# A table rewritten for its first sixteen strips ahead of the first pass over it

## The chip, the cores and the metric

The kernel runs on one core of a Trainium2 chip. A core has five engines with queues of their own: TensorE (PE, matmuls; its weight loads are shown as PEld), VectorE (DVE), ScalarE (ACT), GpSimd (POOL) and SyncE (SP, which here only issues DMAs). Sixteen DMA engines move data between device memory and the on-chip memory, whichever queue has issued the transfer. The metric is the time of one execution on the device in microseconds, as the median of several runs.

## The reference

A layer of a graph network: 12500 nodes with 128 features, 200000 edges sorted by their target `dst`, four types of edges with a weight matrix and a bias each.

```python
h = jnp.maximum(_layernorm(x, axis=-1), 0.0)
# edge by edge, with xs = h[src]:
for i in range(W.shape[0]):
    mask = (edge_types == i)[:, None]
    msgs = msgs + jnp.where(mask, xs @ W[i] + b[i], 0.0)
out = x + jax.ops.segment_sum(msgs, dst, num_segments=N)
```

The targets are drawn as a square of a uniform number, so low nodes have very many edges and high nodes few.

## The kernel before, in words

**Two ways to the sums.** The edges stand in 1563 chunks of 128. The first 576 chunks go to the few heavy targets and are done densely: for a target and a type, it is counted how often each of the 12500 sources occurs, and the counts are multiplied with the table of `h`. The other 987 chunks are gathered: POOL fetches the 128 rows of a chunk from the table by an indirect DMA (L622, tile `hm`, ten buffers of two chunks), PE sums them by a one-hot matrix (L675), weighs the sums with the four matrices (L701), and DVE adds them to a ring of output columns (L764). Groups have 16 chunks and eight parts of two chunks; the first three groups use rows of `x` instead of the table (tile `hx`, the "raw" groups, L733 and L746).

**Two tables.** `h` is written first, as `htab` in device memory: for each node 128 numbers in three 16-bit parts (one float16, two bfloat16), 768 bytes. Gathers read `htab`. The dense passes, but for the first, read a second table, `dtab`: the float16 part and the two others added up as one 32-bit number, 768 bytes too. The table is cut into 98 blocks of 128 nodes, three blocks to a strip: 33 strips of 288 KB (the last is shorter).

**Dense work** goes by batches of targets: the first batch has 29 units (three targets each), eighteen have 31. `count` makes a batch's counts: DVE builds two one-hot matrices for a slot of 128 edges (L1103, L1113), PE multiplies them (L1138), ACT casts the result into the tile `counts` (L1146). Each count has three 8-bit digits in one 32-bit word. `multiply` then makes a pass over the table for the batch, while the next batch is counted. In a pass over `dtab`, two strips form a run: six matmuls with the float16 part and the counts read as 8-bit floats (L1252), then six with the 32-bit part and the counts decoded by ACT (L1206 in `decode`, tile `dec`, L1244). In the first pass, each block takes three matmuls with the three 16-bit parts and the 8-bit counts (L1274) and no decoding.

**Where `dtab` comes from.** The first pass makes it on its way: when a strip has been multiplied, `keep` copies its float16 part on ACT (L1220), adds the other two on DVE (L1221), both into a buffer of the pool `decp` (four buffers, the same in which counts are decoded), and issues the store on ACT's queue (L1222), one strip late. Strips are loaded by SP into seven buffers `hs` (L1263 in the first pass, L1237 later). The pool of these buffers was opened in `end_raws`, at the end of the raw groups' work. At the end of a pass ACT copies the product, `sd` (L1290).

**Order.** PE, DVE and ACT run in the order in which the program is written. The loop over groups (from group 3, `gi == RAW`) writes it: at each of the eight parts of a group it takes as much dense work as `pace` allows. The pace counts columns of matmuls: a batch's counting and pass have a price in columns (`counting_columns`, `passing_columns`), and all of it is spread over 57 groups so that each group with its own columns has the same sum, some 34 thousand dense columns a group, 37 thousand in the narrow early ones. A pass costs `3 * units * PARTS * NW * NT` columns, with FIRST_PASS in place of PARTS for the first. Counting of the first batch, with 29 slots, has no pass beside it and is priced at ALONE = 3.5 times its columns, 39.8 thousand. By the plan it ends in group 4; the first pass and the counting of batch 1 begin there. In `dense_work`, a pass is opened by three calls of its generator (one decode each where it decodes); the first stands ahead of the next batch's first slot, and the pass trails that batch's counting by BEHIND = 0.15.

```python
for n in range(DECS - 1):
    decode(n)
    if n:
        settle(sds)
    yield 0.0
```

Of the kernel before, what the change touches and what calls it, by code (L numbers as in the profile page):

```python
# [36 lines left out]
BF16 = mybir.dt.bfloat16  # L37
F16 = mybir.dt.float16
F8 = mybir.dt.float8e4
F32R = mybir.dt.float32r  # L40
# [4 lines left out]
ALU = mybir.AluOpType  # L45
# [5 lines left out]
P = 128  # L51
# [7 lines left out]
UB = 31  # L59
MANY = 16  # L60
HB = 3
# [17 lines left out]
RUN = 2  # L79
UP = 4096.0  # L80
PARTS = 2.05
FIRST_PASS = 4.4
ALONE = 3.5
RAW_WORK = 20000.0
RAW_ADDS = 12
# [4 lines left out]
def kernel(  # L90
# [1093 lines left out]
    checks = []  # L1184

    sds = []

    def multiply(now):
        vs, counts = now
        nu = len(vs)  # L1190

        first = vs is batches[0]
        table = (htab if first else dtab).rearrange("(p j) f -> p j f", j=NW)
        split = dtab.rearrange("(p j) f -> p j f", j=NW)
        nv = 3 * nu * NT
        by_digit = counts.bitcast(U8)
        counts = counts.bitcast(F8)
        parts = [(j0, min(j0 + HB, NW)) for j0 in range(0, NW, HB)]
        decoded = {}

        def decode(n):
            j0, j1 = n * DS, min(n * DS + DS, NW)
            if first or j0 >= NW:
                return
            decoded[n] = decp.tile([P, DS, 3 * UB * NT], F32R, name="dec")
            nc.scalar.activation(  # L1206
                decoded[n][:, : j1 - j0, :nv].rearrange("p j (m v) -> p j m v", m=3),
                by_digit[:, j0:j1, : nu * NT * 4].rearrange("p j (v m) -> p j m v", m=4)[:, :, :3, :],
                AF.Copy,
                scale=2.0**-9,  # L1210
            )

        stores = []

        def keep(n, hs):
            j0, j1 = parts[n]
            both = decp.tile([P, DS, 3 * UB * NT], F32R, name="dec").rearrange("p j v -> p (j v)")
            both = both[:, : HB * D3 // 2].rearrange("p (j f) -> p j f", j=HB)[:, : j1 - j0]
            rest = hs.bitcast(BF16)[:, : j1 - j0]
            nc.scalar.copy(both.bitcast(F16)[:, :, :D], hs[:, : j1 - j0, :D])  # L1220
            nc.vector.tensor_tensor(both[:, :, D // 2 :], rest[:, :, D : 2 * D], rest[:, :, 2 * D :], ALU.add)  # L1221
            stores.append(lambda: nc.scalar.dma_start(split[:, j0:j1, :], both.bitcast(F16)))  # L1222
            if len(stores) > 1:
                stores.pop(0)()

        for n in range(DECS - 1):
            decode(n)
            if n:
# [1 line left out]
            yield 0.0  # L1230
        pa = a_ps.tile([P, 512], F32, name="pa")
        to = pa[:, :nv]
        for n in range(0, 0 if first else len(parts), RUN):
            run = []
            for j0, j1 in parts[n : n + RUN]:
                hs = rooms[2].tile([P, HB, D3], F16, name="hs")
                nc.sync.dma_start(hs[:, : j1 - j0, :], table[:, j0:j1, :])  # L1237
                run += [(j, hs[:, j - j0, :]) for j in range(j0, j1)]
            for c in (0, 1):
                if n + RUN + c not in decoded:  # L1240
# [17 lines left out]
                        )  # L1258
                if run[-1][0] + c < NW:
                    yield (run[0][0] + len(run) * (1 + c) / 2) / NW  # L1260
        for n, (j0, j1) in enumerate(parts if first else ()):
            hs = rooms[2].tile([P, HB, D3], F16, name="hs")
            nc.sync.dma_start(hs[:, : j1 - j0, :], table[:, j0:j1, :])  # L1263
            for ja in range(j0, j1, DS):
                js = range(ja, min(ja + DS, j1))
                todo = []
                for j in js:
                    of = counts[:, j, : nu * NT * 4].rearrange("p (v m) -> p m v", m=4)[:, :3, :]
                    todo.append((0, j, hs[:, j - j0, :D], of))
                    for c in (1, 2):  # L1270
                        todo.append((c, j, hs.bitcast(BF16)[:, j - j0, c * D : (c + 1) * D], of))
                todo.sort(key=lambda one: one[0])
                for n_done, (c, j, left, right) in enumerate(todo):
                    nc.tensor.matmul(  # L1274
                        to.rearrange("p (m v) -> p m v", m=3),
                        left,
                        right,
                        start=(j == 0 and c == 0),
                        stop=(js[-1] == NW - 1 and n_done == len(todo) - 1),
                    )  # L1280
                if js[-1] + 1 < NW:
                    yield (js[-1] + 1) / NW
            keep(n, hs)
        for store in stores:
            store()
        sds.append(lambda: end())

        def end():
# [309 lines left out]
    for gi, (t0, g) in list(enumerate(zip(starts, sizes)))[RAW:]:  # L1598
# [234 lines left out]
```

## Time and profile before

| | us |
|---|---|
| median of 3 runs | 1305.66 |
| the runs | 1305.32, 1305.66, 1309.93 |
| the profiled execution | 1311.28 |
| its span, first to last instruction | 1309.6 |
| first matmul of the first pass (L1274) | 164.5 |
| its copy `sd` | 247.6 |
| last copy `sd`, of the nineteenth batch | 1276.5 |

The page of the profile gives busy time by engine, the span in 40 equal slices of about 33 us (each digit the busy share in tenths), the chain of work that ended last, and groups of equal instructions with their line, tile names, number, busy time, mean duration in ns, and the idle time of the engine ahead of them with what ended it. The timeline lists instructions in order of time: start, duration, engine, line, operation, output and input, and in brackets the idle time before it. The window view gives each engine's busy time in a stretch, with the granted PE clock and the mean share of the DMA engines. "issue" is idle time for which the profile shows no cause.

### The profile page before, as it was taken

The page shows a single profiled execution, that of the slowest core. Times are in us where ns is not written, and L with a number is a line of the kernel's source. Part 1 is how long each engine was busy: PE and PEld are TensorE (multiplying, and loading weights), DVE is VectorE, ACT ScalarE, POOL GpSimd, SP SyncE. Part 2 cuts the span into 40 slices and gives each one's busy share as a digit, 9 for nine tenths or more (in the row PEclk, how much of TensorE's full clock was granted, in tenths as well). Part 3 has the DMA queues.
Part 4 walks back from the last instruction along what each step waited for, and adds up shares of the span by engine and source line. Part 5 has one row for each costly group of instructions (what it writes and reads, how often), then busy time and mean ns, then how long its engine had stood idle before and what let it go on. Part 6 is the DMA issues. An engine that isn't in the chain of part 4 may idle for free.

```text
span 1309.6 us, 30266 instructions
## 1 busy us (share of the span) xinstructions
PE 1227.2 (94%) x9190; PEld 878.9 (67%) x9190; DVE 1072.4 (82%) x5214; ACT 1064.0 (81%) x1814; POOL 954.0 (73%) x1028
## 2 busy tenths in 40 slices
PE   4887898799999999999999999999999999999996
PEld 1345655577777777777777776777777777777775
DVE  8996487897898987989888887879888797978454
ACT  6795644498988989899898988889888898888881
POOL 6727577777777777777777777777777777777772
PEclk9895689799999999999999999999999999999998
DMA  8644289888888888888787877878788788787982
GB/s 252 215 172 145 60 253 335 287 281 254 268 270 253 258 273 259 260 256 275 245 268 243 286 236 254 259 231 276 235 269 250 242 268 252 254 246 242 290 277 83
DMA packets 184229, 321.75 MB, mean 246 GB/s; under 512 B 30100, under 2 KB 82253, under 8 KB 184061
## 3 DMA queue, kind: packets, MB, share of 16 engines
q1 hardware_dynamic: 132701, 214.63, 50.2%
q0 software_dynamic: 46608, 95.52, 25.6%
q10 hardware_dynamic: 4752, 9.64, 1.9%
q8 instruction: 72, 1.18, 0.4%
q14 instruction: 96, 0.79, 0.2%
HBM read 293.99 MB, written 25.67 MB: 244 GB/s over the span
## 4 chain that ended last, share of the span: by engine, by line
PE 81%; ACT 8%; DVE 6%; DMA 2%; issue 2%; SPq 0%; DVEq 0%; ACTq 0%
PE pa L1244 22%; PE pa L1252 22%; PE pt L1138 11%; PE py L701 8%; PE ps L675 7%; ACT dec L1206 2%; PE pt L1297 2%; DMA dtab<-dec 1%; PE pa L1274 1%; DVE ring L764 1%; ACT h L540 1%; PE ps L733 1%; DVE o L1103 1%; PE pt L986 1%; DVE o L1113 1%
## 5 line engine op out<-in xcount | busy, mean ns | idle before, releaser
L622 POOL DMA_INDIRECT hm<-htab,srcT x939 | 900.8, 959 | 311.6 <-issue 194.1
L1206 ACT ACTIVATE dec<-counts 128x1116 fp32r<-128x1116 uint8 (+1 forms) x594 | 676.1, 1162 | 10.2 <-PE pa L1244 7.6
L1103 DVE TENSOR_SCALAR o<-iota_w,hkT 128x392 bf16<-128x392 f16 x1051 | 429.3, 408 | 114.8 <-PE pt L1138 113.3
L1244 PE MATMUL pa<-dec,hs 128*128 128x372 f32 x1764 | 389.9, 355 | 0.0
L1252 PE MATMUL pa<-counts,hs 128*128 128x372 fp8e4 x1764 | 342.5, 327 | 7.8 <-ACT sd L1290 7.8
L1146 ACT CAST counts<-pt 128x396 int32<-128x396 f32 x587 | 292.1, 523 | 39.5 <-PE pt L1138 15.2
L1244 PEld LDWEIGHTS pa<-dec,hs 128*128 128x128 f32 x1764 | 302.3, 188 | 15.6 <-issue 0.3
L1138 PE MATMUL pt<-o,o 128*128 128x396 bf16 x1051 | 280.1, 338 | 12.9 <-DVE o L1113 11.3
L1252 PEld LDWEIGHTS <-hs 128*128 128x128 f16 x1764 | 165.3, 97 | 121.3 <-issue 12.3
L1113 DVE TENSOR_SCALAR o<-iota_b,loT,byT 128x128 bf16<-128x128 bf16 x746 | 245.5, 329 | 0.0
L764 DVE TENSOR_TENSOR ring<-ring,py 128x14 f32 (+6 forms) x912 | 158.4, 174 | 58.0 <-issue 13.0
L665 ACT ACTIVATE sb<-ps 128x224 f32<-128x224 f32 (+7 forms) x235 | 102.6, 437 | 104.7 <-PE py L701 87.5
L675 PEld LDWEIGHTS <-hm 128*128 128x128 f16 x2817 | 142.9, 99 | 66.4 <-issue 13.3
L675 PE MATMUL ps<-oh,hm 128*128 128x56 bf16 (+7 forms) x2817 | 174.0, 198 | 1.6 <-DMA hm<-htab,srcT 1.6
L640 DVE TENSOR_SCALAR oh<-iota_b,keyT 128x56 bf16<-128x56 bf16 (+7 forms) x939 | 161.0, 261 | 6.8 <-PE ps L675 6.8
L701 PE MATMUL py<-sb,wsb 128*128 128x224 f32 (+6 forms) x456 | 122.3, 412 | 0.0
L1138 PEld LDWEIGHTS <-o 128*128 128x128 bf16 x1051 | 82.3, 98 | 55.5 <-DVE o L1113 16.0
L701 PEld LDWEIGHTS py<-sb,wsb 128*128 128x128 f32 x456 | 83.3, 193 | 26.4 <-ACT counts L1146 4.3
L1113 DVE TENSOR_SCALAR o<-iota_b,loT 128x128 bf16<-128x128 bf16 x305 | 83.0, 272 | 0.0
L606 POOL DMA_INDIRECT hx<-in_x_dram,srcT x48 | 46.8, 974 | 22.6 <-issue 9.3
L1274 PE MATMUL pa<-counts,hs 128*128 128x348 fp8e4 x294 | 53.0, 325 | 0.4 <-DMA hs<-htab 0.4
L696 ACT CAST cnt<-pt 128x224 bf16<-128x224 f32 (+10 forms) x61 | 25.7, 421 | 26.1 <-PE pt L692 24.5
(253 smaller groups left out, 789.8 us busy)
## 6 DMA issues: line engine op xcount, KB each, us to landing
hs<-dtab SPq DMA_DIRECT2D x576, 288.0 KB
hm<-htab,srcT POOLq DMA_INDIRECT x939
htab<-h SPq DMA_DIRECT2D x32, 288.0 KB
hs<-htab SPq DMA_DIRECT2D x32, 288.0 KB
dtab<-dec ACTq DMA_DIRECT2D x32, 288.0 KB
xo<-in_x_dram SPq DMA_DIRECT2D x23, 256.0 KB
out_dram<-xo SPq DMA_DIRECT2D x23, 256.0 KB
hm<-in_x_dram SPq DMA_DIRECT2D x18, 192.0 KB
```

Of the source, the lines that this page charges most:

```text
L622: one = nc.gpsimd.indirect_dma_start(out=hm[:, (i - h0) * D3 : (i - h0 + 1) * D3], out_offset=None, in_=htab, in_offset=bass.IndirectOffse ...
L640: nc.vector.tensor_scalar(oh[:, i, :], iota_b[:, :K], keyf[:, at : at + 1], None, ALU.is_equal)
L675: nc.tensor.matmul(ps[:, i - i0, :], rows(i, c), oh[:, i, :], start=(c == 0), stop=(c == 2))
L701: nc.tensor.matmul(py[:, :g, :], wsb[:, t, :], sb[0][:, :g, t, :], start=False, stop=(t == NT - 1))
L764: nc.vector.tensor_tensor(to, to, of(i), ALU.add)
L1103: one = nc.vector.tensor_scalar(o2[:, k, :NB].rearrange("p (r n) -> p r n", r=ROWS), iota_w, hkT[:, s : s + 1], None, ALU.is_equal)
L1113: one = nc.vector.tensor_scalar(o1[:, k], iota_b, loT[:, s : s + 1], by, ALU.is_equal, ALU.mult)
L1138: one = nc.tensor.matmul(pb, o1, o2, start=first, stop=last)
L1146: lambda i=i, pb=pb: nc.scalar.copy(counts[:, :, i * NT : (i + 1) * NT], pb.rearrange("p (b t) -> p b t", t=NT))
L1206: nc.scalar.activation(decoded[n][:, : j1 - j0, :nv].rearrange("p j (m v) -> p j m v", m=3), by_digit[:, j0:j1, : nu * NT * 4].rearrange(" ...
L1244: nc.tensor.matmul(to.rearrange("p (m v) -> p m v", m=3), row.bitcast(F32R)[:, D // 2 :], decoded[j // DS][:, j % DS, :nv].rearrange("p (m ...
L1252: nc.tensor.matmul(to.rearrange("p (m v) -> p m v", m=3), row[:, :D], counts[:, j, : nu * NT * 4].rearrange("p (v m) -> p m v", m=4)[:, :3 ...
```

## The change

A generator `rewrite` loads the first 16 strips of `htab` and rewrites them into `dtab` before the first pass, by the same `keep`. The loop over groups calls it once per part, from group 3 on; a call loads one strip and rewrites the strip loaded four calls earlier. The last of its twenty calls also issues the last store. When `multiply` is started for the first batch, it runs what is left of the generator to its end, ahead of its first decode. The first pass then takes strips 0 to 15 from `dtab`, in runs of two strips with decoded counts as later passes do, and strips 16 to 32 from `htab` in three parts as before, rewriting each behind its matmuls. The pool `hsp` is opened beside `decp`, before the loop over groups. The price of the first pass in `pace` falls from 4.4 to 3.6.

```diff
-FIRST_PASS = 4.4
+FIRST_PASS = 3.6
+EARLY = 16
+AHEAD = 4
...
+    strips = [(j0, min(j0 + HB, NW)) for j0 in range(0, NW, HB)]
+    stores = []
...
+    def keep(j0, j1, hs):
+        both = decp.tile([P, DS, 3 * UB * NT], F32R, name="dec").rearrange("p j v -> p (j v)")
+        both = both[:, : HB * D3 // 2].rearrange("p (j f) -> p j f", j=HB)[:, : j1 - j0]
+        rest = hs.bitcast(BF16)[:, : j1 - j0]
+        nc.scalar.copy(both.bitcast(F16)[:, :, :D], hs[:, : j1 - j0, :D])
+        nc.vector.tensor_tensor(both[:, :, D // 2 :], rest[:, :, D : 2 * D], rest[:, :, 2 * D :], ALU.add)
+        stores.append(lambda: nc.scalar.dma_start(blocks_of(dtab)[:, j0:j1, :], both.bitcast(F16)))
+        if len(stores) > 1:
+            stores.pop(0)()
+
+    def rewrite():
+
+        coming = []
+        for n in range(EARLY + AHEAD):
+            if n < EARLY:
+                j0, j1 = strips[n]
+                hs = hsp.tile([P, HB, D3], F16, name="hs")
+                nc.sync.dma_start(hs[:, : j1 - j0, :], blocks_of(htab)[:, j0:j1, :])
+                coming.append((j0, j1, hs))
+            if n >= AHEAD:
+                keep(*coming.pop(0))
+            yield True
+        stores.pop(0)()
...
         first = vs is batches[0]
+        for _ in writing if first else ():
+            pass
+        straight = EARLY if first else len(strips)
...
-            if first or j0 >= NW:
+            if n >= straight:
                 return
...
-        for n in range(0, 0 if first else len(parts), RUN):
+        for n in range(0, straight, RUN):
...
-        for n, (j0, j1) in enumerate(parts if first else ()):
+        for j0, j1 in strips[straight:]:
...
+            keep(j0, j1, hs)
...
     decp = counting.enter_context(tc.tile_pool(name="decp", bufs=DECS, side="right"))
+    hsp = counting.enter_context(tc.tile_pool(name="hsp", bufs=STREAM, side="right"))
+    writing = rewrite()
...
-        rooms.append(counting.enter_context(tc.tile_pool(name="hsp", bufs=STREAM, side="right")))
...
             late, tails[:] = list(tails), []
+            next(writing, None)
             while work and spent < pace(gi, part):
```

More of the change, by code (lines that the diff above doesn't have):

```diff
@@ L1197, in multiply @@
         counts = counts.bitcast(F8)
-        parts = [(j0, min(j0 + HB, NW)) for j0 in range(0, NW, HB)]
         decoded = {}
@@ L1211, in decode @@
             )
[L1213 to L1224, printed above, removed]
         for n in range(DECS - 1):
@@ L1260, in multiply @@
                     yield (run[0][0] + len(run) * (1 + c) / 2) / NW
-        for n, (j0, j1) in enumerate(parts if first else ()):
[L1262 to L1283, printed above, removed]
+        for j0, j1 in strips[straight:]:
+            hs = hsp.tile([P, HB, D3], F16, name="hs")
+            nc.sync.dma_start(hs[:, : j1 - j0, :], blocks_of(htab)[:, j0:j1, :])
+            todo = []
+            for c in range(3):
+                for j in range(j0, j1):
+                    left = hs.bitcast(BF16) if c else hs
+                    todo.append((left[:, j - j0, c * D : (c + 1) * D], counts[:, j, : nu * NT * 4].rearrange("p (v m) -> p m v", m=4)[:, :3, :]))
+            for i, (left, right) in enumerate(todo):
+                nc.tensor.matmul(
+                    to.rearrange("p (m v) -> p m v", m=3), left, right, start=False, stop=(j1 == NW and i == len(todo) - 1)
+                )
+            if j1 < NW:
+                yield j1 / NW
+            keep(j0, j1, hs)
         for store in stores:
             store()
+        stores.clear()
         sds.append(lambda: end())
```

10 lines of the change are left out of this document (5 added, 5 removed).

## The prediction, made before the changed kernel was run

> **What bounds the kernel now.** I read the page first, for what is busy all the time.
>
> ```profile
> span 1309.6 us, 30266 instructions
> PE   4887898799999999999999999999999999999996
> POOL 6727577777777777777777777777777777777772
> L622 POOL DMA_INDIRECT hm<-htab,srcT x939 | 900.8, 959 | 311.6 <-issue 194.1
> L675 PE MATMUL ps<-oh,hm 128*128 128x56 bf16 (+7 forms) x2817 | 174.0, 198 | 1.6 <-DMA hm<-htab,srcT 1.6
> L701 PE MATMUL py<-sb,wsb 128*128 128x224 f32 (+6 forms) x456 | 122.3, 412 | 0.0
> ```
>
> PE is at nine tenths from the eighth slice on. POOL never goes over seven, which looks like room. The timeline of POOL says otherwise, so it came second; then the window view of the gathers.
>
> ```profile
> 168.23 0.94 POOL L622 DMA_INDIRECT hm<-htab,srcT  x1 [0.55 <-PE ps L675]
> ...
> 1286.71 0.94 POOL L622 DMA_INDIRECT hm<-htab,srcT  x1 [0.30 <-DVE flag L893]
> 1287.96 0.95 POOL L622 DMA_INDIRECT hm<-htab,srcT  x1 [0.30 <-issue]
> ```
>
> ```profile
> 80.00:168.20 88.20, 51.46 (x48) 0.65 0.35 106
> 168.20:1290.00 1121.80, 849.39 (x891) 0.99 0.83 260
> ```
>
> A gather starts every 1.25 us: 0.95 of work and 0.30 that nothing shortens. From 168.23 on, 891 starts have 890 gaps, 1112.5 us at that pace, and took 1119.7. So POOL works without a break to 1288.9 and loses 7 us on the way. **PE and POOL bound the kernel together**; POOL may run 20 gathers (ten buffers of two) ahead of L675. The wait of 0.55 at 168.23 is the last that PE imposes: until then POOL is held back by PE, and what delays PE there delays POOL's whole row.
>
> Third, the window view by stages: counting of batch 0 (up to the first matmul of the first pass), strips 1 to 16, strips 17 to 33, what follows up to the copy `sd`, and a steady stretch for comparison. Columns: PE, PEld, DVE, ACT, POOL busy (instructions), granted clock, DMA share, GB/s.
>
> ```profile
> 150.60:164.50 13.90, 9.03 (x69) 4.94 (x68) 13.55 (x60) 10.56 (x28) 10.55 (x12) 0.87 0.28 76
> 164.50:201.50 37.00, 34.52 (x293) 21.91 (x292) 31.48 (x153) 15.99 (x41) 28.47 (x28) 0.90 0.84 265
> 201.50:238.40 36.90, 31.60 (x291) 20.95 (x290) 26.88 (x124) 15.46 (x40) 28.43 (x28) 1.00 1.00 347
> 238.40:247.60 9.20, 3.47 (x22) 1.27 (x19) 7.00 (x31) 3.98 (x7) 6.97 (x8) 0.59 0.99 327
> 350.00:450.00 100.00, 99.01 (x796) 73.72 (x795) 91.08 (x447) 91.64 (x146) 75.59 (x81) 1.00 0.84 264
> ```
>
> Counting of batch 0 is bound by DVE (13.55 of 13.90), with DMA at a share of 0.28. The second half of the pass is bound by DMA (share 1.00). The steady stretch is full on PE and over 90% on ACT and DVE.
>
> **Rewriting ahead: strips 0 to 9.** Loads, copies, adds and stores are the same instructions, moved. Keeps 0 to 3 stand at parts 4 to 7 of group 3, keeps 4 to 9 at parts 0 to 5 of group 4, by one step per part and a lag of four.
>
> ```profile
> 150.57 0.42 DVE L1103 TENSOR_SCALAR o<-iota_w,hkT 128x392 bf16<-128x392 f16 x1 [13.86 <-PE pt L1138]
> ...
> 177.19 0.55 DVE L1221 TENSOR_TENSOR dec<-hs 128x384 fp32r<-128x384 bf16 x1
> ```
>
> ```profile
> 168.10 0.51 ACT L1220 COPY dec<-hs 128x384 f16<-128x384 f16 x1
> 168.50 0.50 ACT L1146 CAST counts<-pt 128x396 int32<-128x396 f32 x1
> ...
> 169.56 0.37 ACTq L1222 DMA_DIRECT2D dtab<-dec  x1
> ```
>
> Keeps 0 to 3 lie in the 13.86 us that DVE waits in group 3: nothing, and 2 us if their copies held up the raw groups' evictions on ACT. Keeps 4 to 9 fall into 150.6 to 164.5. An add takes DVE 0.47 (the chain's piece below), a copy ACT 0.40 (168.10 to 168.50) and a store's issue 0.37. Six keeps are 2.8 us of DVE and 4.6 of ACT, whose own idle there is 3.3. I take DVE's **2.8**; bounds 0 and 4.6.
>
> **The drain.** `multiply` empties the rest of the generator before its first decode. Batch 0's counting ends at 39.8 thousand columns; the pace allows 39.2 before part 5 of group 4, where 14 of 20 steps are done. So six keeps (10 to 15) come in one block. Behind them in order are decode 0 on ACT, the casts of batch 1's slots, and on PE the fifth slot and the first matmul of the pass. Four buffers `dec` serve six keeps and the decodes, so copy 14 waits until store 10 has landed.
>
> ```profile
> 164.20 0.51 PE L1138 MATMUL pt<-o,o 128*128 128x396 bf16 x1 [0.45 <-DVE o L1113]
> 164.51 2.82 PE L1274 MATMUL pa<-counts,hs 128*128 128x348 fp8e4 x9
> 167.53 0.42 PE L675 MATMUL ps<-oh,hm 128*128 128x48 bf16 x6
> ```
>
> ```profile
> 176.32 0.15 PE ps L675 x6
> ...
> 192.21 4.65 DMA dtab<-dec
> ...
> 232.60 0.47 DVE dec L1221
> ```
>
> ```profile
> 255.90 2.16 ACT L1206 ACTIVATE dec<-counts 128x1116 fp32r<-128x1116 uint8 x2 [0.41 <-PE pa L1244]
> ```
>
> From the last one-hot for batch 1's slots (now about when the pass starts): add 10 0.47, store 10 0.37, landing, copy 14 and copy 15 with a store between them 1.17, two stores 0.74, decode 0 1.08, a cast 0.40, a slot 0.17: 4.4 us and a landing. No row shows a landing with quiet queues. From below, 288 KB at the 347 GB/s of the third stage are 0.85 us; from above stands the 4.65 in the full queue. DMA is at 0.28 here; I take 2.8, in the middle: **7.2 us**, bounds 5.3 and 9.1. [...]
>
> So the pass starts at about 174.5, 10 us later. PE is idle for most of it.
>
> **Strips 0 to 15 in two parts.** The chain's pieces give the matmuls at full clock.
>
> ```profile
> 173.52 1.38 PE pa L1274 x9
> 174.99 1.33 PE py L701 x8
> ...
> 253.98 0.99 PE pa L1252 x6
> 255.29 1.02 PE pa L1244 x6
> ```
>
> A strip costs PE 1.38 now, and three of each new kind 0.50 and 0.51: 16 strips fall from 22.1 to 16.1, 6.0 us saved. Left out besides are 16 adds (7.5 of DVE), copies and issues (12.3 of ACT). Added are 16 decodes, 17.3 of ACT. ACT's 15.99 become 26.9 (less 6.4 for copies; issues are not counted as busy). At the 91.64% that ACT reaches when PE is full, that is 29.4 us in place of 37.0: **-7.6**, bounds -6.0 (PE's saving alone) and -10.1 (ACT without a gap). DMA hides: the reads move from `htab` to `dtab`, the stores are gone.
>
> **Strips 16 to 32 and the end** keep their instructions, 46.1 us (201.5 to 247.6), DMA-bound. They start without the stores of strips 1 to 16 in the queue and have about 0.4 group less among them. I take **-2.5**; bounds 0, since the bytes of these strips are the same, and -8 (nine transfers of 288 KB less in the queue, at the 347 GB/s of that stage).
>
> **Pace.** FIRST_PASS down by 0.8 takes 27.3 thousand columns out of a plan of 37 thousand per early group, so 0.74 group fewer stands beside the pass and comes later. A group's sums are 8 x 0.15 and 1.33, 2.5 us early; over the run 174.0/2817x48 + 122.3/456x8 = 5.1. **+2**, bounds 1.9 and 3.8.
>
> **Sum:** 2.8 + 7.2 - 7.6 - 2.5 + 2 = +1.9 us: span 1311.5. The profiled execution took 1311.28 around its span of 1309.6, above the median of 1305.66; the change is put on the median, which gives **1307.6**, no difference that a measurement of this kernel tells from none (about 0.5%, 6.5 us).
>
> **Does POOL allow it?** L675 at 167.53 comes after the first half run (1.0) and moves by 8; POOL has no slack there, so its row moves by 8. Some of its 7 us loss comes back.
>
> ```profile
> 177.14 1.45 POOL L622 DMA_INDIRECT hm<-htab,srcT  x1 [0.31 <-issue]
> 178.90 0.94 POOL L622 DMA_INDIRECT hm<-htab,srcT  x1 [0.30 <-DMA hm<-htab,srcT]
> ...
> 1297.94 0.31 PE L675 MATMUL ps<-oh,hm 128*128 128x104 bf16 x3
> ```
>
> The gather at 177.14 is 0.5 longer, just beside the add at 177.19. Half the adds now meet a waiting POOL: 3 back of 7, bounds 0 and 7. The Trainium skill, "SBUF — State Buffer", section "SBUF: two separate sides", says that a DVE operation in a two-port mode locks GpSimd out of writing descriptors; the trace agrees with these two rows. POOL then ends 5 us later. Today 10.0 us lie between the start of the last gather and the last L675; 0.95 and a landing of 2.8 are needed, so 6.2 are free. POOL does not bind the forecast, but from about 1 us faster than before it would.
>
> **Rivals.** *Faster: a short drain.* Keeps 4 to 9 hidden (0), landing 0.85 (5.3), strips 0 to 15 at -10.1, the rest at -8, pace +2: -10.8. POOL's row then moves by 3.3, less 3, and the last L675 cannot come before 1290.1: at best -7.8. That gives 1297.9. For it: DMA at 0.28 before the pass. Against: ACT's queue stands still at every wait for a store.
>
> *Slower: ACT's queue.* It holds copies, store issues behind adds, decodes and casts in order. Landing at 4.65 (+1.9), keeps 4 to 9 at ACT's price (+1.8) and strips 0 to 15 at -6.0 (+1.6) give +7.2, 1312.9. It decides from a landing of about 4 us. For it: ACT is over 90% busy wherever it decodes. Against: quiet queues.
>
> *The change doesn't do what it says:* strips 0 to 15 stay at 37 us because ACT's decodes take what PE saves. +9.5, 1315.2. Against: the steady loop is the same code at a full PE. Its 19 copies `sd` (18 passes between) show the rate:
>
> ```profile
> L1290 ACT ACTIVATE sd<-pa x19: 442/473/502, 247.6 to 1276.5; 128x372 f32<-128x372 f32 x18, 128x348 f32<-128x348 f32 x1
> ```
>
> 57.2 us for 33 strips, 1.73 each, 27.7 for 16.
>
> **Chances.** Forecast 0.53, faster rival 0.22, ACT's queue 0.20, no gain in the pass 0.05. Faster by over 0.5%: 0.20 (the first rival but 0.02); slower: 0.24 (the last two but 0.02, and 0.01 of the forecast); within: 0.56. The range goes from the short drain to the last rival: 1298 to 1316, with one in ten left out at each end.
>
> **What would show it.** Right: first L1252 of the first pass near 174.5; a block of six copies on ACT with waits for `dtab` stores ahead of it; POOL waiting some 8 us for L675 between 165 and 176; sixteen strips in about 29 us; `sd` near 247.5; a lead of POOL at the end of about 7 us in place of 10. Wrong: a pass that starts before 170, or DVE and ACT stalls in strips 0 to 15 that leave PE under 85%. If the strips 16 to 32 run under 30 us, the backlog was worth more than I gave it.

## The result, and the profile after

The changed kernel took 1315.87 us in the median (1314.48 to 1317.85, 8 runs), the kernel before in the same set 1309.26 (1305.32 to 1312.3, 8 runs): a ratio of 1.0055, 95% interval 1.0038 to 1.0071. Forecast was +1.9 us, no difference that can be told; the change costs 6.6 us. Every later ratio is to the kernel before in its own set. (e1 to e18 are the runs below.) The three sets e1 to e4, e13 to e16, and e17 with e18 ran on two of the four chips that the sets had, where the kernel before takes 1574 to 1576 us because PE stands still every few microseconds; their times are compared only among themselves.

From the page of the changed kernel, the rows that answer to those of before:

```profile
span 1314.7 us, 30217 instructions
PE   4887769799999999999999999999999999999996
POOL 6737547777777777777777777777777777777773
L624 POOL DMA_INDIRECT hm<-htab,srcT x939 | 897.1, 955 | 323.6 <-issue 193.2
L677 PE MATMUL ps<-oh,hm 128*128 128x56 bf16 (+7 forms) x2817 | 173.4, 198 | 0.0
```

(L624, L677, L1115, L1140, L1148 are the lines that stood two higher in the kernel before; the copy, the add and the store of `keep` are now L1199, L1200, L1201, the decode L1237, the matmuls L1270, L1262 and, in three parts, L1288, the copy `sd` L1301.) PE does less, with a hole in its fifth and sixth slices (7 and 6 where 8 and 9 stood). The window view, by stages: from the last row of the raw groups (the copy at 149.3) to the first matmul of the first pass, to the first `sd`, to the last `sd`, to the end. The columns are those of the prediction.

```profile
149.30:177.20 27.90, 8.63 (x63) 4.78 (x61) 22.29 (x83) 15.70 (x39) 14.17 (x14) 0.67 0.92 307
177.20:246.70 69.50, 59.38 (x521) 41.35 (x519) 55.05 (x271) 41.73 (x84) 50.81 (x53) 0.92 0.90 299
246.70:1281.50 1034.80, 1016.26 (x7876) 747.93 (x7877) 859.86 (x4209) 905.96 (x1409) 782.80 (x828) 1.00 0.82 257
1281.50:1314.70 33.20, 20.41 (x176) 16.06 (x173) 14.99 (x78) 4.93 (x12) 10.97 (x12) 0.86 0.32 88
```

The same stages in the kernel before:

```profile
151.00:164.50 13.50, 8.63 (x65) 4.60 (x63) 13.15 (x59) 10.16 (x28) 10.15 (x12) 0.88 0.29 78
164.50:247.60 83.10, 69.59 (x602) 44.13 (x600) 65.36 (x306) 35.42 (x86) 63.87 (x63) 0.91 0.93 308
247.60:1276.50 1028.90, 1015.21 (x7844) 747.80 (x7845) 861.02 (x4202) 906.51 (x1406) 778.63 (x821) 1.00 0.83 258
```

The first stage grew by 14.4 us, the pass fell by 13.6, the long stretch of eighteen passes grew by 5.9. In the first stage PE works the same 8.63 us; DVE has 9.1 us more, and DMA, at 0.29 before, is at 0.92: the rewriting's own loads and stores fill the queues (5 and 12 are issued in this stage), and with them seven loads of strips that the pass will read. What ACT waits for in that stage is in its view of waits (line, releaser: total, times, longest):

```profile
ACT dec L1199 <- DMA dtab<-dec: 6.3, 4, 2.8
ACT counts L1148 <- PE pt L1140: 2.7, 1, 2.7
ACT counts L1148 <- DVE dec L1200: 2.7, 1, 2.7
ACT dec L1199 <- DVE dec L1200: 2.1, 1, 2.1
ACT dec L1237 <- DMA dtab<-dec: 1.0, 1, 1.0
```

Copies wait 6.3 us for stores that free their buffers, decode 0 another 1.0; 4.8 us are waits for an add on DVE, by which ACT's queue is held at a store. The chain that ended last shows one such landing (the time from a store's issue until its bytes have arrived) whole, and what stands behind it up to the pass:

```profile
168.43 0.35 ACTq L1201
...
168.90 4.88 DMA dtab<-dec
173.86 0.52 ACT dec L1199
174.41 0.57 DVE dec L1200
175.00 0.35 ACTq L1201
...
175.40 1.07 ACT dec L1237
176.47 0.39 ACT counts L1148
...
176.90 0.49 PE pt L1140
177.39 0.87 PE pa L1270 x3
```

A landing is 4.88 us where I took 2.8. While PE is out, POOL fills its ten buffers and stops:

```profile
166.49 0.95 POOL L624 DMA_INDIRECT hm<-htab,srcT  x1 [0.30 <-issue]
180.03 0.94 POOL L624 DMA_INDIRECT hm<-htab,srcT  x1 [12.60 <-PE ps L677]
...
1294.87 0.94 POOL L624 DMA_INDIRECT hm<-htab,srcT  x1 [0.30 <-issue]
```

### The profile page after: what moved, and what is told of

The parts are those of the page before. It is cut to its first block, busy times and chain, and to the rows that moved or that the text cites. A ratio compares the mean times of both kernels' runs of the same rounds, so it can differ in the third digit from the quotient of the medians.

```text
span 1314.7 us, 30217 instructions
## 1 busy us (share of the span) xinstructions
PE 1214.9 (92%) x9142; PEld 874.2 (66%) x9142; DVE 1072.0 (82%) x5214; ACT 1076.8 (82%) x1830; POOL 950.9 (72%) x1028
## 4 chain that ended last, share of the span: by engine, by line
PE 78%; ACT 8%; DVE 7%; DMA 4%; issue 2%; DVEq 0%; SPq 0%; ACTq 0%
PE pa L1262 22%; PE pa L1270 21%; PE pt L1140 11%; PE py L703 8%; PE ps L677 7%; ACT dec L1237 3%; DMA dtab<-dec 2%; PE pt L1308 2%; DVE ring L766 1%; DVE o L1105 1%; DVE o L1115 1%; PE ps L735 1%; ACT counts L1148 1%; ACT h L542 1%; PE pt L988 1%
## 5 line engine op out<-in xcount | busy, mean ns | idle before, releaser
L624 POOL DMA_INDIRECT hm<-htab,srcT x939 | 897.1, 955 | 323.6 <-issue 193.2
L1237 ACT ACTIVATE dec<-counts 128x1116 fp32r<-128x1116 uint8 (+2 forms) x610 | 696.1, 1163 | 9.0 <-DMA dtab<-dec 6.1
L1262 PE MATMUL pa<-dec,hs 128*128 128x372 f32 (+1 forms) x1812 | 400.6, 355 | 0.2 <-ACT dec L1237 0.2
L1270 PE MATMUL pa<-counts,hs 128*128 128x372 fp8e4 (+1 forms) x1812 | 351.8, 327 | 11.2 <-ACT sd L1301 9.6
L1262 PEld LDWEIGHTS pa<-dec,hs 128*128 128x128 f32 x1812 | 310.8, 189 | 16.3 <-issue 0.8
L1148 ACT CAST counts<-pt 128x396 int32<-128x396 f32 x587 | 295.2, 524 | 28.7 <-PE pt L1140 13.2
L1140 PE MATMUL pt<-o,o 128*128 128x396 bf16 x1051 | 279.2, 337 | 29.3 <-DVE o L1115 17.1
L1270 PEld LDWEIGHTS <-hs 128*128 128x128 f16 x1812 | 169.8, 97 | 136.5 <-issue 14.5
L1115 DVE TENSOR_SCALAR o<-iota_b,loT,byT 128x128 bf16<-128x128 bf16 x746 | 244.0, 327 | 0.0
L677 PEld LDWEIGHTS <-hm 128*128 128x128 f16 x2817 | 141.7, 99 | 63.7 <-issue 13.7
L677 PE MATMUL ps<-oh,hm 128*128 128x56 bf16 (+7 forms) x2817 | 173.4, 198 | 0.0
L1140 PEld LDWEIGHTS <-o 128*128 128x128 bf16 x1051 | 83.4, 98 | 63.0 <-DVE o L1115 22.6
L703 PEld LDWEIGHTS py<-sb,wsb 128*128 128x128 f32 x456 | 83.1, 193 | 24.6 <-ACT dec L1199 2.0
L1115 DVE TENSOR_SCALAR o<-iota_b,loT 128x128 bf16<-128x128 bf16 x305 | 82.7, 271 | 0.0
L698 ACT CAST cnt<-pt 128x224 bf16<-128x224 f32 (+10 forms) x61 | 25.7, 422 | 30.9 <-PE pt L694 29.1
L542 ACT ACTIVATE h<-hm,nmrt,rstdt 128x128 f32<-128x128 f32 x98 | 42.2, 491 | 1.1 <-DVE nmrt L537 1.0
```

Source lines behind the costliest of these rows:

```text
L624: one = nc.gpsimd.indirect_dma_start(out=hm[:, (i - h0) * D3 : (i - h0 + 1) * D3], out_offset=None, in_=htab, in_offset=bass.IndirectOffse ...
L677: nc.tensor.matmul(ps[:, i - i0, :], rows(i, c), oh[:, i, :], start=(c == 0), stop=(c == 2))
L703: nc.tensor.matmul(py[:, :g, :], wsb[:, t, :], sb[0][:, :g, t, :], start=False, stop=(t == NT - 1))
L1115: one = nc.vector.tensor_scalar(o1[:, k], iota_b, loT[:, s : s + 1], by, ALU.is_equal, ALU.mult)
L1140: one = nc.tensor.matmul(pb, o1, o2, start=first, stop=last)
L1148: lambda i=i, pb=pb: nc.scalar.copy(counts[:, :, i * NT : (i + 1) * NT], pb.rearrange("p (b t) -> p b t", t=NT))
```

## The experiments

A first table, of the profiles of the two sets that ran like the first comparison, and of the two kernels compared there: stage lengths in us, each from the first and last rows that bound it (first gather; last raw row; first matmul of the first pass; first and last `sd`; end), and the ratio.

| kernel | raw | to the pass | pass | `sd` to `sd` | end | sum from the first gather | ratio (95%) |
|---|---|---|---|---|---|---|---|
| before | 58.0 | 13.5 | 83.1 | 1028.9 | 33.1 | 1216.6 | |
| before again, e5 | 58.0 | 13.5 | 84.0 | 1028.3 | 30.2 | 1214.0 | |
| pace alone, e6 | 57.9 | 14.1 | 82.2 | 1031.9 | 30.2 | 1216.3 | 1.0007 (0.9991 to 1.0022) |
| early, three parts, e7 | 56.3 | 27.6 | 73.0 | 1032.2 | 32.0 | 1221.1 | 1.0059 (1.0040 to 1.0078) |
| changed | 57.6 | 27.9 | 69.5 | 1034.8 | 33.2 | 1223.0 | 1.0055 (1.0038 to 1.0071) |
| changed again, e9 | 57.8 | 28.5 | 69.6 | 1033.7 | 34.6 | 1224.2 | 1.0068 (1.0050 to 1.0087) |
| ten strips, old pace, e8 | 57.9 | 19.7 | 77.0 | 1028.1 | 32.1 | 1214.8 | 0.9991 (0.9978 to 1.0003) |
| two steps a part, e10 | 61.7 | 17.2 | 70.0 | 1033.4 | 32.2 | 1214.5 | 1.0007 (0.9996 to 1.0019) |
| two steps, old pace, e11 | 61.7 | 16.4 | 75.9 | 1029.8 | 34.7 | 1218.5 | 1.0013 (0.9998 to 1.0028) |
| three steps, old pace, e12 | 70.0 | 13.5 | 75.7 | 1027.2 | 33.4 | 1219.8 | 1.0043 (1.0026 to 1.0060) |

The two profiles of the kernel before differ by 2.6 us in the sum, nearly all of it in the last stage; their other stages agree within 0.9. Smaller differences than these are not read.

**First set: the changed kernel, its pace undone, its drain removed in two ways.**

The changed kernel as it is (no edit).

> The changed kernel itself, beside the others of this set. Both theories: 1.004 to 1.007 of the time of before; the first L1270 of the first pass near 177, POOL's long wait near 180 some 12 us, and 1034 to 1036 us between the first and the last `sd`. If the 5.9 us by which that stretch is longer than before are a matter of one execution and not of the kernel, this run shows 1029 to 1032 there.

```diff
-FIRST_PASS = 3.6
+FIRST_PASS = 4.4
```

> The changed kernel with FIRST_PASS 4.4 as before: the pace alone undone. Theory A (the longer stretch from the first to the last `sd`, 1034.8 us against 1028.9, comes of the pace, which lets more groups of gathers lie behind the dense work): that stretch falls back to 1029 to 1031 and the time lies 3 to 6 us under the changed kernel's, about that of before. Theory B (the stretch is longer because POOL's lead was spent in the drain and the pace has no part in it): the stretch stays at 1033 to 1036, and the time stays within 2 us of the changed kernel's. In both, the drain ahead of the first pass stays: the first L1270 at 176 to 178.

```diff
             next(writing, None)
+            next(writing, None)
```

> The changed kernel with two steps of the rewriting in each part of the raw groups instead of one: all 20 steps are done before the first pass is reached and no drain is left. Drain theory (the 12.7 us by which the first pass starts later are the keeps 10 to 15 in a row on ACT, each waiting for the landing of the store that frees its buffer): the first L1270 at 165 to 169, POOL's wait of 12.6 us mostly gone, and the time 4 to 8 us under the changed kernel's, a little below that of before. Rival (the queues are full of the rewriting's own bytes, wherever these lie): the raw stage before it becomes longer by as much, the first L1270 stays at 174 to 178, and the time stays within 2 us of the changed kernel's.

```diff
-EARLY = 16
+EARLY = 10
```

> The changed kernel with 10 strips rewritten ahead instead of 16: 14 steps, which all fall into the parts before the first pass, so that no drain is left, and 23 strips go in three parts. Drain theory: the first L1270 at 165 to 169; the ten strips in two parts gain some 4 to 6 us on the 23 us that they took in three, so the first `sd` comes 4 to 8 us before the changed kernel's 246.7, and the time is 3 to 8 us under it. Rival (a dense start that comes earlier is only taken back by the gathers of POOL, which set the end): the first `sd` comes earlier but the time stays within 2 us of the changed kernel's.

Here the kernel before took 1575.67 us. Ratios: e1 1.0086 (1.0053 to 1.0119), e2 1.0069 (1.0044 to 1.0094), e3 1.0043 (1.0024 to 1.0062), e4 1.0027 (1.0008 to 1.0046). None of the absolute expectations (177, 1034) could be met in this set; two rows of PE's timeline of e1 show why:

```profile
701.12 1.15 PE L1270 MATMUL pa<-counts,hs 128*128 128x372 fp8e4 x6 [1.37 <-issue]
...
703.78 0.34 PE L1140 MATMUL pt<-o,o 128*128 128x396 bf16 x1 [1.50 <-issue]
```

PE is idle for 1.4 us with nothing to wait for, again and again (busy 83% of the span in place of 92%), and POOL then waits for PE all the way. What can be read is the comparison within the set. Without the drain the first matmul comes 18.0 (e3) and 19.9 us (e4) behind the last raw row in place of 28.8 (e1), and the medians are 6.3 and 7.5 us lower than that of e1, though the intervals of e1 and e3 just overlap; neither comes down to the kernel before. The pace undone puts the first `sd` 14 us later (306.2 in place of 292.2) and shortens the rest by 9, with no difference in time that can be told from none. So the drain theory had its direction; of theory A on the pace, the shorter stretch came and the 3 to 6 us did not.

**Second set: the steps of the change, one upon the other.** The kernel before (no edit); the kernel before with the new pace alone; the changed kernel without its two parts; the changed kernel with ten strips and the old pace.

> The kernel before itself, for a profile beside those of this set and the set before it. If the first set's longer times (1575.67 us for the kernel before instead of 1309.26) belong to the chip and not to a kernel, PE's instructions keep their durations here too (L1244 and L1252 333 and 326 ns in the middle) and the added time is idle time of PE that ends on nothing the profile names. The part that the change touches is read between the last row of the raw groups, L1573, and the first L1274: 13.5 us in the profile of before.

```diff
-FIRST_PASS = 4.4
+FIRST_PASS = 3.6
```

> The kernel before with FIRST_PASS 3.6 as in the changed one: the pace alone done. Theory A (the pace costs some 3 to 5 us, by gathers that are left for later): 1.002 to 1.004 of before. Theory B (the pace only moves work between the first pass and the later groups): within 0.15% of before, with the first `sd` some 10 us earlier and the stretch from the first to the last `sd` longer by as much.

```diff
-        straight = EARLY if first else len(strips)
+        straight = 0 if first else len(strips)
...
-                    to.rearrange("p (m v) -> p m v", m=3), left, right, start=False, stop=(j1 == NW and i == len(todo) - 1)
+                    to.rearrange("p (m v) -> p m v", m=3), left, right, start=(j0 == 0 and i == 0), stop=(j1 == NW and i == len(todo) - 1)
...
-            keep(j0, j1, hs)
+            if j0 >= EARLY * HB:
+                keep(j0, j1, hs)
```

> The changed kernel's rewriting ahead, its drain and its pace, but the first pass takes all 33 strips from htab in three parts, and rewrites only strips 16 to 32 after use; so the gain of the two parts is taken away and all the costs stay, less the sixteen decodes on ACT. Theory C (the two parts gain the 10 to 12 us that the first sixteen strips showed, 25.7 us against 37.0, and the drain takes them back): 1.011 to 1.016 of before. Rival D (gathers and not PE's work decide behind the first pass, so that the gain in PE's work is not carried to the end): 1.004 to 1.008, about the changed kernel's.

```diff
-FIRST_PASS = 3.6
-EARLY = 16
+FIRST_PASS = 4.4
+EARLY = 10
```

> Ten strips rewritten ahead and FIRST_PASS 4.4: no drain and the pace of before. If drain and pace were all that the change loses, this one gains the ten strips' 4 to 6 us: 0.995 to 0.998 of before. If the rewriting costs also where it lies beside the raw groups (its keeps on DVE, its loads and stores in the queues), 1.000 to 1.004, as with ten strips and the new pace (1.0027).

The kernel before took 1310.04 us here and showed the old 13.5 us ahead of the pass, so the longer times belong to where the first set ran. **The pace** makes the long stretch 3.0 to 3.6 us longer and the pass 0.9 to 1.8 shorter; in time it is 1.0007, within the interval no change: theory B, though the first `sd` didn't move by 10 us as it said. **The rewriting ahead** (e7 against e6) costs 13.5 us ahead of the pass and gives 9.2 back in it; from 1.0007 to 1.0059, it is the whole loss. **The two parts** (changed kernel against e7) shorten the pass by 3.5 us and nothing else; 1.0055 and 1.0068 against 1.0059 tell no gain. That is rival D by its ratio, while theory C's 10 us are not there. Ten strips with the old pace (e8) lie at 0.9991, between the two readings that were set for them. The window rows of e7, to be held beside those of the changed kernel, and then the pass of e6:

```profile
150.80:178.40 27.60, 8.68 (x62) 4.81 (x61) 21.40 (x80) 14.79 (x39) 13.05 (x14) 0.68 0.92 302
178.40:251.40 73.00, 66.14 (x569) 43.17 (x567) 54.09 (x264) 28.27 (x69) 53.04 (x55) 0.96 0.89 289
```

```profile
165.80:248.00 82.20, 68.35 (x569) 43.70 (x567) 64.89 (x294) 34.68 (x82) 62.13 (x65) 0.92 0.94 318
```

e6 and e7 do the same 569 matmuls in the pass. In e7 it is 9.2 us shorter: PE is idle for 6.9 us instead of 13.9, since sixteen adds and sixteen stores have left the pass, and its work takes 2.2 less, at a granted clock of 0.96 instead of 0.92. The two parts then take 6.8 us of PE's work away (66.14 to 59.38, 48 matmuls), and PE's idle time rises from 6.9 to 10.1. Half of the saving is idle time at once. Where, the two halves of the pass show (strips 0 to 15, which end at the 145th matmul in three parts, and the rest), of e7 and of the changed kernel:

```profile
178.40:210.00 31.60, 31.60 (x277) 20.68 (x276) 23.73 (x129) 10.39 (x28) 21.39 (x23) 0.96 0.78 231
210.00:251.40 41.40, 34.54 (x298) 22.50 (x294) 30.36 (x135) 17.87 (x41) 31.66 (x33) 0.96 0.98 333
```

```profile
177.20:202.90 25.70, 25.70 (x227) 19.77 (x226) 20.00 (x114) 23.51 (x43) 17.38 (x19) 0.90 0.79 254
202.90:246.70 43.80, 33.68 (x300) 21.59 (x296) 35.05 (x159) 18.22 (x41) 33.43 (x35) 0.93 0.96 325
```

The first half is all PE in both, and the two parts make it 5.9 us shorter. The second half has the same strips and the same seventeen stores, its DMA share is 0.96 to 0.98, and it is 2.4 us longer: ACT waits there 12.5 us for landings, 9.6 in e7.

**Third set: the rewriting where DVE is idle.** The changed kernel again (no edit), with two steps a part (as e3), the same with the old pace, and three steps with the old pace.

> The changed kernel once more, beside the kernels of this set. The stretch from the first to the last `sd` was 1028.9, 1028.3 and 1028.1 us in the three kernels with the pace of 4.4 and 1031.9, 1032.2 and 1034.8 in those with 3.6, the last being the changed kernel. If its 2.6 us above the other two belong to the two parts, they are here again (1034 to 1036); if to the one execution, 1031 to 1033. Time 1.004 to 1.007 of before.

> The changed kernel with two steps of the rewriting in each part, where PE's instructions are not held up as they were in the first set. Theory A (the rewriting costs because twelve of its sixteen keeps lie where DVE is the engine that all wait for, behind the last row of the raw groups): the steps now lie mostly in the first raw group, where DVE is busy 1.71 of 10 us; from the last raw row L1586 to the first L1270 16 to 19 us instead of 27.9, POOL's wait of 12.6 us down to under 5, and 0.999 to 1.002 of before. Theory B (the rewriting costs wherever it lies): the raw group grows by what the drain loses, 62 us or more from the first gather L624 to L1586 instead of 57.6, and 1.004 to 1.006 of before.

> The same with FIRST_PASS 4.4. Theory A: 0.997 to 1.000 of before, since the pace is worth about 0.001 (e6_pace_alone 1.0007) to 0.002; the stretch from the first to the last `sd` 1028 to 1029. Theory B: 1.003 to 1.005. If POOL's gathers, which run at a fixed 1.25 us once the pass has begun, set the end: the last gather L624 lies 1196 us behind the first one, as in e8_ten_strips_old_pace, however much less PE has to do, and the time is that of before within 0.2%.

```diff
             next(writing, None)
+            next(writing, None)
+            next(writing, None)
...
-FIRST_PASS = 3.6
+FIRST_PASS = 4.4
```

> Three steps in each part and FIRST_PASS 4.4: all twenty steps are done within the first raw group. Theory A: from L1586 to the first L1270 13 to 16 us as in before (13.5), and 0.995 to 0.999 of before. Theory B: 63 us or more from the first gather to L1586, and 1.002 to 1.005. If the gathers set the end, within 0.2% of the run with two steps.

Two steps bring the stage ahead of the pass from 28 to 17 us and the time from 1.0068 to 1.0007: the drain's cost is gone, as theory A said. But the raw groups grow by 3.7 us, and by 12 with three steps, as theory B said. With two steps and the old pace the time is 1.0013, between the two theories; with three, it is 1.0043 though nothing is left ahead of the pass. (The changed kernel again, e9, has 1033.7 from the first to the last `sd`, between its two readings.) ACT's timeline of e12 shows what it stands at:

```profile
131.25 0.51 ACT L1199 COPY dec<-hs 128x384 f16<-128x384 f16 x1 [1.38 <-DMA dtab<-dec]
...
136.50 0.51 ACT L1199 COPY dec<-hs 128x384 f16<-128x384 f16 x1 [1.42 <-DMA dtab<-dec]
...
138.51 0.51 ACT L1199 COPY dec<-hs 128x384 f16<-128x384 f16 x1 [1.49 <-DMA dtab<-dec]
```

The same wait for a buffer, now ahead of the raw groups' evictions. In its raw stage of 70.0 us ACT waits 5.7 us for landings and 3.3 for adds on DVE; in e10, 3.9 for adds alone; the changed kernel and the kernel before have neither wait there. So the rewriting's price is not only where it lies, but that ACT's queue stands at a landing or at a store that waits for its add.

**Fourth and fifth set: POOL or PE.** Six gathers fewer in the changed kernel and in the one before, six more in the one before, 48 matmuls more in the one before; then the first and the last once more.

```diff
+FEWER = 8 * 16
...
         for h0 in range(0, g, HG):
+            if t0 == FEWER and h0 % (2 * HG) and h0 > HG:
+                got.append(got[-1])
+                continue
             hm = hpool.tile([P, HG * D3], F16, name="hm")
```

> The changed kernel with six gathers fewer: in the group at column 128 three tiles of rows are not gathered, and the tile before each is summed up in its place (so three pairs of columns of that group are summed from other rows; PE, DVE and ACT do as much as before). 6 x 1.25 us = 7.5 us of POOL's chain go, and nothing of PE's. Theory P (POOL's gathers, which run at a fixed 1.25 us from the first pass on and never wait again, set the end; the drain stopped them for 12.6 us): the last gather comes 7.5 us earlier behind the first one (1195.7 instead of 1203.2 to 1205.3) and the time falls by 3 to 7.5 us, to 1.000 to 1.003 of before. Theory E (PE's work and its idle time set the end): the time stays at 1.005 to 1.007.

> The kernel before with the same six gathers fewer. If POOL's chain sets its end too: up to 7.5 us less, 0.995 to 0.998. If PE sets the end of the kernel before and POOL only that of the changed one: within 0.1% of before.

```diff
+MORE = 8 * 16
...
             got.append(hm)
+            if t0 == MORE and h0 % (2 * HG) and h0 > HG:
+                hm = hpool.tile([P, HG * D3], F16, name="hm")
...
```

> The kernel before with six gathers more: three tiles of rows in the group at column 128 are gathered once more into buffers that nobody reads. It puts 7.5 us on POOL's chain and nothing on PE's, as the drain's stop does without the rest of the change. Theory P: 5 to 8 us more, 1.004 to 1.006 of before, with the last gather 1202 to 1204 us behind the first. Theory E: within 0.15% of before.

```diff
+                    if n < 16:
+                        todo.append((3, j, hs.bitcast(BF16)[:, j - j0, 2 * D : 3 * D], of))
```

> The kernel before with a fourth matmul for each block of strips 0 to 15 of the first pass, a repeat of the third (the sum of these blocks then has its last part twice): 48 matmuls more, which at the 0.141 us that one takes (41.4 us from the first L1274 to the last for 294 of them at 0.141 if nothing lay between) put 6.8 us on PE's work where the change takes as many away. Theory E: 1.003 to 1.005 of before. Theory P: within 0.15%, since the gathers are not held up.

> The changed kernel with six gathers fewer, as in e13_six_gathers_fewer_changed (three pairs of columns of the group at column 128 are summed from other rows), which was run where PE's instructions are held up for some 1.3 us every 6 us and POOL waits for PE to the end, so that POOL's chain bounds nothing there. Where POOL's gathers run at their fixed 1.25 us from the first pass to the last gather: theory P (they set the end) 1.000 to 1.003 of before, the last gather some 1196 to 1198 us behind the first; theory E (PE sets the end) 1.005 to 1.007.

> The kernel before with 48 matmuls more in the first pass, as in e16_four_parts_before (the blocks of strips 0 to 15 have their last part summed twice). Theory P: the last gather stays 1195 to 1197 us behind the first, and the time is within 0.15% of before. Theory E: 6.8 us more of PE's work, 1.003 to 1.005.

Both sets ran where PE stands still, and POOL waits there to the end, so they don't test theory P as it was meant. Six gathers fewer: the changed kernel at 1.0091 (1.0063 to 1.0118) and 1.0080 (1.0052 to 1.0107), against 1.0086 in e1; the one before at 1.0000 (0.9981 to 1.0019). So the loss is there in full where POOL waits for PE throughout; gathers are not needed to carry it to the end. Six more: 1.0044 (1.0018 to 1.0069), the number of theory P, but where POOL waits for PE nearly all along (561 us idle before its gathers, 313 in e5); the first pass, beside which these gathers lie there, takes 116.8 us in place of the 109.1 and 110.3 of e16 and e18. Whether the gathers' time or the three buffers that they take from ten do it, no run tells. 48 matmuls more: 1.0012 (0.9995 to 1.0028) and 1.0020 (0.9994 to 1.0047), 1.9 and 3.2 us for 6.8 us of PE's work, with intervals that hold 0, and of which the second just holds 6.8.

What the profiles of the other sets say of POOL: in the first pass, kernels with the old pace wait for gathers. In e11 it is, between 180 and 300 us,

```profile
PE ps L677 <- DMA hm<-htab,srcT: 10.4, 11, 2.3
```

and 10.3 in e12, 4.8 in e8, 1.6 and 0.8 in the two profiles of the kernel before. With the new pace, e6, e7, e10 and the changed kernel have none, and e9 one of 2.1. So with the old pace a pass that is given less to multiply meets POOL: e11's takes 75.9 us where e10's takes 70.0, and the totals tell no difference. In the long stretch of the changed kernel, one wait of a weight load for a gather is listed, of 0.2 us. At the end, there is one such wait in the kernels of the table, in e10, whose last gather and last weight load for it are

```profile
1289.03 0.95 POOL L624 DMA_INDIRECT hm<-htab,srcT  x1 [0.30 <-PE pt L799]
```

```profile
1292.91 0.16 PEld L677 LDWEIGHTS <-hm 128*128 128x128 f16 x3 [0.26 <-DMA hm<-htab,srcT]
```

So PE had that gather's rows 3.9 us after its start. In the changed kernel 7.1 lie there (1294.87 to the last L677 at 1301.99): by this one row POOL leaves it 3.2 us, and does not set its end. e10 comes to its first `sd` 6 us sooner after the first gather than the kernel before (148.9 against 154.6) and at the end meets POOL, by a wait of 0.26.

## Why the prediction was wrong, step by step

By the table, the span from the first gather grew by 6.4 us where the sum had 1.9. **The step that failed is the price of the work ahead of the pass: 2.8 + 7.2 = 10.0 us forecast, 14.4 measured.** Strips 0 to 15 gained 11.3 for 7.6, strips 16 to 32 gained 2.3 for 2.5, the stretch behind cost 5.9 for 2, and the raw groups and the end together -0.3 for nothing. Step by step:

- **Keeps 0 to 3 cost nothing:** right. The raw groups take 57.6 us in place of 58.0.
- **Keeps 4 to 9, "I take DVE's 2.8; bounds 0 and 4.6": this step failed.** e8 has these keeps and of the drain only its last store, which `multiply` issues ahead of decode 0 (the generator has it behind its last `yield`, so it is not in the last of the calls). Its stage is 6.2 us longer (19.7 against 13.5); 1.1 of it is decode 0, which I had booked with the drain, so the keeps took 5.1. The chain of the changed kernel agrees: its last one-hot ahead of the drain's adds ends at 167.9, 9.3 us before the first matmul, which leaves 5.1 of the 14.4. I priced DVE's adds and ACT's copies each on its own engine. DVE is the one that is full in e8's stage (18.32 of 19.70), and six adds are 3.4 of it, 0.56 each instead of 0.47. The remaining 1.7 is not taken apart by a run; what the rows show is a wait between the two engines: a store on ACT's queue waits for its add, the add stands in DVE's order behind one-hot matrices, and decode and cast wait behind the store. The window row of that stage, and ACT's rows at its end:

```profile
152.50:172.20 19.70, 8.91 (x67) 4.77 (x65) 18.32 (x75) 12.70 (x33) 13.00 (x14) 0.76 0.85 260
```

```profile
170.04 0.35 ACTq L1201 DMA_DIRECT2D dtab<-dec  x1
170.44 1.07 ACT L1237 ACTIVATE dec<-counts 128x1044 fp32r<-128x1044 uint8 x1 [3.94 <-DVE dec L1200]
171.42 0.47 ACT L1148 CAST counts<-pt 128x396 int32<-128x396 f32 x1
```

During most of the 3.94 us that ACT waits, DVE makes one-hot matrices that are needed in any case (166.5 to 169.5 in its timeline); the pass is delayed by the add and by what comes behind it.

- **The drain, 7.2 with decode 0; bounds 5.3 and 9.1:** 9.3 to 9.9 (27.9 and 28.5 against e8's 19.7, and the 1.1 of decode 0). The landing in it was 4.88 us and not 2.8, which is the 2.1 us up to 9.3; the other pieces of the chain come to 4.4 as forecast, though an add of 0.57 ahead of the last store, which I had left out, stands there for a copy and a store that were not in the row. "DMA is at 0.28 here" was read from the kernel before; with the change's own transfers it is 0.92. And the buffers were short before copy 14: copies 11, 13, 14 and 15 all waited for a landing.
- **Start of the pass:** 177.2 in place of 174.5, with the six copies and POOL's wait as described (12.6 us in place of 8).
- **Strips 0 to 15, -7.6, for the two parts:** the strips took 25.7 us (177.2 to the first L1288 at 202.9), less than the 29.4 forecast. 5.9 of the gain belong to the two parts (31.6 in e7), where I had 6.0 as PE's saving alone; most of the rest comes with the keeps that left (35.8 in e6, 31.6 in e7). ACT, by whose load I set the 29.4, was busy for 23.5 us and held up nothing: PE works without a gap.
- **Strips 16 to 32, -2.5:** -2.3 (202.9 to 246.7, 43.8 against 46.1), but as the sum of two things: -5.0 with the keeps that left (46.4 in e6, 41.4 in e7) and +2.4 with the two parts, which I had not seen. For the whole pass the keeps give 9.2 and the two parts 3.5.
- **Pace, +2:** the long stretch grew by 5.9. e6 shows 3.0 to 3.6 for the pace, within my bounds, and 1.8 to 2.1 when what its pass gives back is taken off: the +2. Of the other 1.8 to 2.9 (e9 and the changed kernel's profile against e6) the cause stays open; it is about as large as either miss ahead of the pass (2.3 and 2.1). e10 with the same work ahead has it too (1033.4), e7 with three parts hasn't (1032.2), and PE's busy time in this stretch varies by 4 us between kernels with nearly the same instructions.
- **POOL:** it does not set the end, as I said, and some of its loss came back (6.9 us later at the last gather after a wait of 12.6, where I had 8 and 5). That its lead at the end is 7.1 us where I said 7 is luck: the last L677 came later than forecast too.

What came is the rival that I gave 0.20, ACT's queue: +7.2 us by its sum, +6.6 by the medians. Its condition, a landing of about 4 us, held, and so did its price ahead of the pass (13.7, measured 14.4); what I set against it, "quiet queues", was a view of the kernel before, and the change is what fills them. That its total is so near is in part luck: it had strips 0 to 15 at -6.0, where -11.3 came, and the stretch behind at +2, where 5.9 came. Shown by runs: the loss lies in the rewriting ahead (e7), it goes when the drain is spread over the parts (e10, one line changed) or left out (e8, with the old pace besides) and shrinks in the first set (e3, e4), it is back where the raw groups wait instead (e12), and the pace alone is not it (e6). No kernel of these beats the one before by more than its interval; the nearest is e8 at 0.9991 (0.9978 to 1.0003).

## What to carry to other kernels

Work that is moved to where an engine is idle brings its waits along: look at what stands behind each of its instructions in the queue, a store that waits for another engine above all. Read the load of a transfer queue with the moved transfers in it, not from the profile in which they lie elsewhere. And a saving on the engine that is busiest over the run is worth only what the stage leaves it: here 6.8 us of matmuls were 5.9 in the strips that had them, where PE works without a gap, and 3.5 in the pass, whose second half has DMA at a share of 0.96 and PE idle for a quarter.

## What the runs showed of the hardware

PE's granted clock follows its work within a few microseconds. The window view of the changed kernel, in steps of 5 us around the drain:

```profile
164.30:169.30 5.00, 1.50 (x4) 0.54 (x5) 4.57 (x16) 0.98 (x2) 2.52 (x3) 0.50 0.91 345
169.30:174.30 5.00, 0.00 (x0) 0.00 (x0) 1.68 (x3) 1.50 (x4) 0.00 (x0) 0.50 0.96 337
...
179.30:184.30 5.00, 5.00 (x42) 4.11 (x39) 3.45 (x20) 5.00 (x11) 3.35 (x4) 0.67 0.51 145
184.30:189.30 5.00, 5.00 (x48) 4.03 (x47) 4.83 (x27) 3.89 (x8) 3.78 (x5) 1.00 0.74 220
```

Idle, PE is granted 0.50, and the pass begins at it: at 0.67, the stretch from 179.3 loses 1.65 us of full-speed work (an estimate). In steps of 0.2 us, the clock is at 0.50 up to 182.4 and at 1.00 from 182.6, that is 5.7 us after PE began to work without a gap, at 176.9. The Trainium skill, "TensorE: Matmul & The Clock Gate", Part 1 on the clock gate, says that half rate is the idle state and that some 3.4 us of activity lift it; the trace agrees on the half rate, and its rise took longer than that. The kernel before begins its pass at 0.50 too and has 1.00 from 168.5, 4.0 us behind its first matmul, so little of the loss is the clock's: some 0.7 us, an estimate from the 1.4 us more at half rate.

The other finding is the two sets of times themselves: the same kernel at 1309 us and, on two chips, at 1575. Of the changed kernel, the profiles are 267 us apart (1314.7 and 1582.1 in e1) with the same instructions, at granted clocks of 0.96 and 0.93. PE is busy for 98 us more in e1 (1312.6 against 1214.9), its idle time that ends on nothing the profile names is 125 us where the other profile has none, and most of the rest are waits for other engines. What holds PE up there was not found.
